# Gelu of four early tiles kept in DRAM until its step, x of the last early tiles loaded sooner, inverse roots of late groups ranked behind normalization

## The chip, the cores and the metric

The kernel runs on one core of a Trainium2 chip. The metric is device time in microseconds (us), the median of the runs. The profile comes from one more execution, recorded by the hardware profiler; its own time is given beside its span.

Engine names in the profile: PE is TensorE's matrix multiplication and PEld its weight load, DVE is VectorE, ACT is ScalarE, POOL is GpSimd, SP is SyncE, which only issues transfers here. A name such as L528 is a line of the kernel.

## The reference

The input x has 4096 rows of 1024 float32 numbers (8 x 512 x 1024). Cut to what matters:

```python
xn   = layernorm(x)                              # each row, eps 1e-5
attn = (w1 @ w2.T) * sparse_mask                 # 1024 x 1024
y    = gelu(xn @ attn + b2)                      # exact gelu; one product, no softmax
w_q  = to_e4m3(weight * 448 / max|weight|)
x_q  = to_e5m2(xn * 57344 / max|xn|)             # one maximum over all of xn
lin  = (x_q @ w_q.T) / x_scale / w_scale + bias
out  = x + y + lin
```

The mask is banded: a column block of 128 needs only rows up to 70 away from it. The scale of the linear layer's input needs the maximum over the whole of xn, so no linear product can start before every row has been normalized or at least measured.

## The kernel before

**Tiles and parts.** The rows are cut into 32 tiles of 128. The first 16 are "early": tile i is loaded once, normalized in place (`normalize` on ACT, L407, or `normalize_gpsimd` on POOL, L416), its row maxima are taken (`row_max`, DVE, L421), PE transposes it in two halves `pt_i_0` and `pt_i_1` (`transpose_one`, L509), ACT or DVE copies them out of PSUM (`evict_transposed` L518, `evict_by_vector` L521), and PE multiplies with the band: `py_i_0` and `py_i_1` (`product_matmul`, L528), each of which must first have been filled with b2 by ACT (`preload`, L525). `gelu_early` (L538) then writes the gelu over the tile of x. Since x itself is gone by then, `add_x` (L541) later fetches it from DRAM once more with an accumulating transfer, which POOL issues. These transfers are released once the gelus and the late maxima (`late_amax`) are done.

The other 16 tiles are "late". In part one they are loaded for their statistics and maxima only: tiles 16 to 23 through a mean and a sum of squares on ACT (`mean_of` L335 and L336, `squares` L339), tiles 24 to 31 through `statistics` on DVE (L330) and a centring on ACT (L349) or POOL (L352). Their slots are given back after the maximum. In part two they are loaded a second time.

**The inverse roots.** 1/sqrt(var) is worked out for groups of tiles (`GROUPS`). Those of tiles 2 to 27 run as eight small operations on POOL (`inverse_root_gpsimd`, L382 to L391), and give `rstd` and `shift` to the normalizations. `root_of_squares` (L397 to L404, POOL) follows the group of 16 to 23. Then `late_amax` and the global maximum of x (PE transposes `pt_x`, L437 and L449) give the scale.

**The weights.** Eight tiles w_0 to w_7 of the linear layer's weight are rounded to fp8 on ACT, DVE (L481, L484) and POOL (L488, L489); a slot becomes free when the second half of its tile has been rounded.

**Part two** starts with the first linear matmul `pf_0_0` (L568) at 132.9 us of the profiled execution. Its steps each take one tile's linear product, in two halves `pf_k_0` and `pf_k_1`, for which there are two PSUM buffers. The products and transposes of the late tiles lie between the linear matmuls. For each half, `total` on DVE scales `pf` and adds the bias (L580), and adds the result to the tile (L583). For an early tile L583 needs the accumulating transfer of `add_x` to have landed; for a late tile it needs POOL's `add_gelu` (L553). `store` issues the output's transfer from ACT's queue. Eight tiles of the mask (`load_mask`) are also read in part two and checked to be zero outside the band (`check_mask`, L604).

**What sets the order.** Every operation is registered with a class `Plan`: engine, planned cost, a rank (the lower goes first among those ready), what it comes after, and which pools it takes from or gives back to. A simulated clock on the planned costs then yields one fixed order for each engine, and the program is emitted in it. Each engine works strictly through its list. An operation placed early waits where it stands, with everything behind it on its engine, whatever the real time is.

The pools that matter are `slot`, 34 tiles of SBUF that hold x, w1, w, xnt, gelu and mask alike, and `stream`, which limits how many late tiles of part one (and mask tiles) are in SBUF at a time. A load waits on SP's queue until its slot is free, with the loads behind it. The order of the loads in part one is written by hand:

```python
ORDER = "eeaaeeeaeeeoaoooooooeeaaesseaesalellssleselllssl"
```

`e` is the next early tile, `s` the next of the late tiles 16 to 23, `l` the next of 24 to 31, `a` the next block of w1, w2 and mask, `o` the next weight tile.

Of the kernel before, what the change touches and what calls it, by code (L numbers as in the profile page):

```python
# [8 lines left out]
F32 = mybir.dt.float32  # L9
# [8 lines left out]
P = 128  # L18
D = 1024
# [4 lines left out]
EARLY = 16  # L24
SLOTS = 34
QUANT = 4
STREAM = 9
LATE = 4

SQUARED = range(EARLY, EARLY + 8)  # L30
# [1 line left out]
BY_SCALAR = (0, 2, 3, 8, 10, 14)  # L32
CENTRED_BY_GPSIMD = range(24, 30)
GROUPS = [(0, 1), (1, 2), (2, 8), (8, 12), (12, 16), (16, 24), (24, 28), (28, 32)]
BY_HALVES = 0
TINY = 1e-36
HALF = 512
# [35 lines left out]

ORDER = "eeaaeeeaeeeoaoooooooeeaaesseaesalellssleselllssl"


def load_order():
# [67 lines left out]
class Plan:  # L147
# [8 lines left out]
    def do(self, engine, cost, rank, emit, *args, lag=0.2, after=(), take=(), free=()):  # L156
        after = [op for op in after if op is not None]
        op = Op(engine, cost, rank, lag, after, take, free, emit, args)
        self.ops.append(op)
        return op  # L160
# [47 lines left out]
def banded_path(  # L208
# [12 lines left out]
    nc = tc.nc  # L221
# [5 lines left out]
    slots = ctx.enter_context(tc.tile_pool(name="slots", bufs=SLOTS))  # L227
    magic_pool = ctx.enter_context(tc.tile_pool(name="magic", bufs=2))
    small = ctx.enter_context(tc.tile_pool(name="small", bufs=2))
    ps_y = ctx.enter_context(tc.tile_pool(name="ps_y", bufs=4, space=psum))  # L230
    ps_f = ctx.enter_context(tc.tile_pool(name="ps_f", bufs=2, space=psum))
    ps_t = ctx.enter_context(tc.tile_pool(name="ps_t", bufs=2, space=psum))
# [5 lines left out]
    def slot(name):  # L238
        return slots.tile([P, D], F32, tag="s", name=name)
# [21 lines left out]
    xs = {}  # L261
# [11 lines left out]
    v = {}  # L273
# [266 lines left out]
    def add_x(i):  # L540
        nc.gpsimd.dma_start(xs[i], x[i * P : (i + 1) * P, :], accum_op=ALU.add)  # L541

    def normalize_late(i):
        xns[i] = slot(f"xn_{i}")
        normalize(i, xns[i])
# [83 lines left out]
    do = plan.do  # L629
    LOAD, T, V, A, G = "load", "tensor", "vector", "scalar", "gpsimd"  # L630
# [21 lines left out]
    for sc in range(NC):  # L652
        mm = do(
            T, 3.6, sc * 0.1, attn_matmuls, sc, after=[attn_ops[c] for c in range(sc + 1)],
            take=("f",), free=("slot",),
# [16 lines left out]
    for lo, hi in GROUPS:  # L672
        group = [stat[i] for i in range(lo, hi)]
        if 0 < lo and hi < TILES:
            op = do(G, 1.9 + 0.18 * (hi - lo), 0, inverse_root_gpsimd, lo, hi, after=group)
        else:
            op = do(V, 0.2, 0, variance, lo, hi, after=group)
            op = do(G, 0.4 + 0.18 * (hi - lo), 0, power, lo, hi, after=(op,))
            op = do(V, 0.6, 0, inverse_root, lo, hi, after=(op,))
        for i in range(lo, hi):  # L680
            root[i] = shifted[i] = op
        if lo == 0 or hi == TILES:
            op = do(V, 0.2, 0 if lo == 0 else 99, shifts, lo, hi, after=(op,))
            for i in range(lo, hi):
                shifted[i] = op
# [9 lines left out]
    for i in range(EARLY, TILES):  # L695
# [8 lines left out]
        after=[maxima[i] for i in SQUARED] + [root[i] for i in SQUARED],  # L704
# [3 lines left out]
        after=[squared] + [maxima[i] for i in range(TILES)] + [root[i] for i in range(TILES)],  # L708
# [19 lines left out]
    for c in range(NC):  # L728
        rank = 5, 4.0, 5.0
        op = do(A, 1.17, rank[0], weight_scaled, c, after=(w_known, w_twice[c]))  # L730
# [5 lines left out]
    known = do(V, 0.2, 0.5, descale, after=(x_known,))  # L736

    products, added = {}, {}
    evicted = {}
    for i in range(EARLY):  # L740
        in_big = i >= EARLY - NC
        for q in range(2):
            op = do(
                T, 0.52, 10 * i - 11 + q, transposes, i, q,
                after=(settled[i], attn_mm[NC - 1] if in_big else None, evicted.get((i, 0))),
                take=("t",) if in_big or q else ("t", "slot"),
            )
            engine, cost, emit = (V, 0.7, evict_by_vector) if q and i in BY_VECTOR else (A, 0.6, evict_transposed)
            evicted[i, q] = do(engine, cost, -2.0, emit, i, q, after=(op,), free=("t",))
        pre = [  # L750
            do(A, 0.62, 1.5 + 0.01 * i, preload, i, h, after=(b2_op,), take=("y",)) for h in range(2)
        ]
        op = evicted[i, 1]
        ends = []
        for piece in band_pieces():
            op = do(
                T, max(0.39, (piece[3] - piece[2]) / 600), 10 * i, product_matmul, i, *piece, lag=0.1 if not piece[-1] else 0.2,
                after=(op, evicted[i, 0], attn_ready[piece[0]], pre[piece[1]]),
            )
            if piece[-1]:  # L760
                ends.append(do(A, 0.62, 0, gelu_early, i, piece[1], after=(op, maxima[i]), free=("y",)))
        products[i] = op

        op = do(LOAD, 2.5, 200 + 10 * i, lambda: None, lag=0.0, after=(*ends, late))
        added[i] = do(G, 1.0, 6 + 0.01 * i, add_x, i, after=(op,), lag=4.0)
# [24 lines left out]
    for s, pair in enumerate(steps):  # L790
        rank = 1000 + 10 * s
        j, nxt = product_in.get(s), turned_in.get(s)
        for k, h in pair:
            if k < EARLY and k not in quantized:
                quantized[k] = do(
                    V, 0.95, 9 + s, quantize, k,
                    after=(x_known, products[k], evicted[k, 1], ends[s - 2] if s > 1 else None),
                    take=("quant",), free=("slot",) if k < EARLY - NC else (),
                )

        op = linear
        for kind, args in interleaved(pair, j is not None, nxt is not None):
            if kind == "product":
                h = args[1]
                op = do(
                    T, 0.335, rank, product_matmul, j, *args, lag=0.0,
                    after=(op, evicted_late[j, 0], evicted_late[j, 1], pre_late[j, h]),
                )
                if args[-1]:
                    last_piece[j, h] = op  # L810
            elif kind == "transpose":
                c, = args
                q, first, last = c // (NC // 2), c % (NC // 2) == 0, c % (NC // 2) == NC // 2 - 1
                op = do(
                    T, 0.13, rank, transpose_one, nxt, c, lag=0.0, after=(op, normal_late[nxt]),
                    take=(("t", "slot") if c == 0 else ("t",)) if first else (),
                    free=("slot",) if c == NC - 1 else (),
                )
                if last:
                    evicted_late[nxt, q] = do(  # L820
                        A, 0.6, 50 + s, evict_transposed, nxt, q, after=(op,), free=("t",)
                    )
            else:
                k, h, c = args
                op = do(
                    T, 0.215, rank, linear_matmul, k, h, c, lag=0.0,
                    after=(op, quantized[k], *(rounded if c == 0 else ())),
                    take=("f",) if c == 0 else (), free=("quant",) if (h, c) == (1, NC - 1) else (),
                )
                if c == NC - 1:  # L830
                    sums[k, h] = op
        linear = op
        ends.append(op)
        if j is not None:
            for h in range(2):
                g = do(
                    A, 0.62, 20 + s, gelu_late, j, h, after=(last_piece[j, h],),
                    take=() if h else ("slot",), free=("y",),
                )
                added_late[j, h] = do(  # L840
                    G, 1.3, 20 + s, add_gelu, j, h, after=(g,), free=("slot",) if h else ()
                )
            quantized[j] = do(
                V, 0.95, 30 + s, quantize, j, after=(x_known, last_piece[j, 0], last_piece[j, 1]),
                take=("quant",), free=("slot",),
            )
        for k, h in pair:
            ready = added_late[k, h] if k >= EARLY else added[k]
            if s == len(steps) - 1:
                op = do(G, 1.3, 20 + s, add_bias, k, h, after=(ready, bias_op))  # L850
                op = do(V, 0.8, 10 + s, total_at_once, k, h, after=(op, sums[k, h], known), free=("f",))
                totals[k, h] = op
            else:
                totals[k, h] = do(
                    V, 1.48, 10 + s, total, k, h, after=(sums[k, h], known, bias_op, ready), free=("f",)
                )
            if s == len(steps) - 1:
                do(A, 0.1, 90, store, k, h, after=(totals[k, h],), lag=4.0)
            elif h == 1:
                stored.append(  # L860
                    do(A, 0.1, 90 + s, store, k, after=(totals[k, 0], totals[k, 1]), lag=4.0,
                       free=("slot",) if k < EARLY else ("slot", "late"))
                )
# [307 lines left out]
```

## Time and profile before

| | us |
|---|---|
| median of 3 runs (lowest to highest) | 321.80 (321.66 to 323.01) |
| the profiled execution | 321.68 |
| its span | 319.8 |
| PE busy | 294.8 |
| DVE, ACT, POOL busy | 232.0, 161.9, 138.0 |
| first linear matmul | 132.94 |

The mean granted clock of PE in the profiled execution is 0.982 of full speed. 69.55 MB are moved in the span.

The profile's page has busy times, the span in 40 slices of 8 us with a digit for the busy tenths of each engine and for the clock granted to PE, the transfer queues (q0 is POOL's, q1 SP's, q10 ACT's), and groups of instructions. The trace behind it answers closer questions: waits by engine and line, a timeline of an engine's instructions (start in us from the span's start, duration, and in brackets how long the engine stood idle before it and for whom), busy times in chosen stretches, and the time from issue to landing of a transfer. A row of the timeline may join neighbouring instructions of one line.

### The profile page before, as it was taken

How to read it: one execution, taken by the hardware profiler on the slowest of the kernel's cores; microseconds unless marked ns; L12 is line 12 of the kernel's file. 1: busy time of each engine (PE TensorE's matmuls, PEld its weight loads, DVE VectorE, ACT ScalarE, POOL GpSimd, SP SyncE). 2: the span in 40 equal slices, each digit the busy share in tenths (PEclk: the TensorE clock that was granted, in tenths of full speed). 3: DMA queues.
4: the chain of work that ended last, by engine and by line, in shares of the span. 5: the costliest groups of instructions: out<-in, count | busy, mean ns of one | idle time of the engine just before them, and what ended most of it. 6: DMA issues, size and time to landing. Idle time of an engine off the chain costs nothing.

```text
span 319.8 us, 4317 instructions
## 1 busy us (share of the span) xinstructions
PE 294.8 (92%) x1530; PEld 217.9 (68%) x1549; DVE 232.0 (73%) x339; ACT 161.9 (51%) x262; POOL 138.0 (43%) x165
## 2 busy tenths in 40 slices
PE   5687879899996899999999999999999999999992
PEld 1665758698894799876766676676667667666651
DVE  3657798899899896358668677767857767676682
ACT  1131578998994799943335244523533452451110
POOL 2402705999998958367443311311321231131160
PEclk9989999999999699999999999999999999999999
DMA  7999999954754190999999999755335223212313
GB/s 243 353 378 380 407 365 388 305 201 167 296 178 151 36 339 20 174 178 225 278 290 307 308 307 372 279 178 184 147 131 198 98 100 133 91 66 107 133 67 139
DMA packets 27693, 69.55 MB, mean 217 GB/s; under 512 B 3344, under 2 KB 12048, under 8 KB 27664
## 3 DMA queue, kind: packets, MB, share of 16 engines
q1 hardware_dynamic: 20320, 42.98, 38.4%
q0 software_dynamic: 2592, 9.44, 14.7%
q10 hardware_dynamic: 4752, 16.78, 13.2%
q8 instruction: 14, 0.23, 0.3%
q14 instruction: 15, 0.12, 0.1%
HBM read 52.41 MB, written 16.78 MB: 216 GB/s over the span
## 4 chain that ended last, share of the span: by engine, by line
PE 64%; DMA 11%; POOL 11%; DVE 6%; SPq 3%; issue 2%; ACT 1%; POOLq 0%; DVEq 0%
PE pf L568 33%; PE py L528 25%; DMA w_sb<-in_w2t_dram 7%; PE pt L509 5%; POOL wq L489 3%; POOL w L488 3%; DMA w<-in_wt_dram 3%; DVE st L330 2%; DMA w<-in_w_dram 2%; DVE magic L481 1%; SPq L290 1%; PE pa L313 1%; DVE magic L484 1%; POOL x L416 1%; POOL g_r L384 1%
## 5 line engine op out<-in xcount | busy, mean ns | idle before, releaser
L568 PE MATMUL pf<-wq,xqts 128*128 128x512 bf16 x493 | 145.6, 379 | 0.8
L528 PE MATMUL py<-attn,xnt 128*128 128x198 f32 (+2 forms) x480 | 114.0, 341 | 2.4 <-ACT py L525 1.2
L528 PEld LDWEIGHTS py<-attn,xnt 128*128 128x128 f32 x480 | 86.8, 190 | 25.2 <-ACT py L525 2.1
L553 POOL TENSOR_TENSOR x<-x,gelu 128x512 f32<-128x512 f32 x32 | 40.7, 1271 | 125.4 <-ACT gelu L550 118.2
L580 DVE SCALAR_TENSOR_TENSOR pf<-pf,descale,bias_bc 128x512 f32<-128x512 f32 x62 | 46.9, 757 | 52.6 <-PE pf L568 50.1
L568 PEld LDWEIGHTS <-xqts 128*128 128x128 fp8e5 x512 | 50.6, 101 | 25.9 <-DVE xqts L561 2.7
L550 ACT ACTIVATE gelu<-py 128x512 f32<-128x512 f32 x32 | 19.1, 597 | 77.9 <-PE py L528 67.5
L518 ACT COPY xnt<-pt 128x512 f32<-128x512 f32 x48 | 27.9, 586 | 37.1 <-PE pt L509 36.3
L583 DVE TENSOR_TENSOR x<-pf,x 128x512 f32<-128x512 f32 x62 | 42.9, 691 | 4.0
L313 PE MATMUL pa<-w_sb,w 128*128 128x268 f32 (+1 forms) x128 | 32.0, 410 | 8.5 <-DMA w_sb<-in_w2t_dram 8.5
L421 DVE TENSOR_REDUCE row_amax<-x 128x1 f32<-128x1024 f32 x32 | 37.6, 1204 | 1.7 <-POOL x L416 1.6
L525 ACT COPY py<-b_bc 128x512 f32<-128x512 f32 x64 | 37.0, 596 | 0.9
L313 PEld LDWEIGHTS pa<-w_sb,w 128*128 128x128 f32 x128 | 26.0, 211 | 14.4 <-issue 6.3
L330 DVE BATCH_NORM_STATS2 st<-x 128x6 f32<-128x512 f32 x48 | 30.2, 671 | 7.5 <-DMA x<-in_x_dram 7.5
L528 PE MATMUL py<-attn,xnt_big 128*128 128x198 f32 (+2 forms) x160 | 34.2, 358 | 0.1
L509 PE MATMUL pt<-ident,xn 128*128 128x128 f32 x128 | 34.0, 273 | 0.2
L528 PEld LDWEIGHTS py<-attn,xnt_big 128*128 128x128 f32 x160 | 28.3, 203 | 2.4
L509 PEld LDWEIGHTS pt<-ident,xn 128*128 128x128 f32 x128 | 17.9, 141 | 14.3 <-ACT xnt L518 0.6
L488 POOL TENSOR_TENSOR w<-w,magic 128x512 f32<-128x512 f32 x16 | 18.9, 1182 | 14.3 <-DVE magic L484 13.9
L509 PE MATMUL pt<-ident,x 128*128 128x128 f32 x128 | 19.8, 283 | 5.4 <-DVE xnt_big L521 2.7
L561 DVE TENSOR_SCALAR xqts<-xnt,x_scale 128x1024 fp8e5<-128x1024 f32 x24 | 24.5, 1026 | 0.0
L509 PEld LDWEIGHTS pt<-ident,x 128*128 128x128 f32 x128 | 14.9, 146 | 9.2 <-DVE xnt_big L521 3.2
(87 smaller groups left out, 233.6 us busy)
## 6 DMA issues: line engine op xcount, KB each, us to landing
x<-in_x_dram SPq DMA_DIRECT2D x48, 512.0 KB, 5.9
out_dram<-x ACTq DMA_DIRECT2D x31, 512.0 KB, 3.3
x<-in_x_dram POOLq DMA_DIRECT2D x16, 512.0 KB, 12.8
w<-in_wt_dram SPq DMA_DIRECT2D x8, 512.0 KB, 9.2
mask<-in_mask_dram SPq DMA_DIRECT2D x8, 512.0 KB, 8.0
w<-in_w_dram SPq DMA_DIRECT2D x7, 512.0 KB, 9.5
w_sb<-in_w2t_dram SPq DMA_DIRECT2D x6, 512.0 KB, 10.3
attn<-in_mask_dram SPq DMA_DIRECT2D x6, 134.0 KB, 9.0
```

The costliest lines, as they stand in the source:

```text
L313: nc.tensor.matmul(pt[:, : hi - lo], w1_sb[:, c, :], w2_sb[:, c, lo:hi], start=(c == 0), stop=(c == NC - 1),)
L330: nc.vector.bn_stats(st[:, h, :], xs[i][:, half(h)])
L421: nc.vector.tensor_reduce(row_amax[:, i : i + 1], xs[i], AX.X, ALU.max, apply_absolute_value=True)
L488: nc.gpsimd.tensor_add(w[:, half(h)], w[:, half(h)], magic[:, half(h)])
L509: nc.tensor.transpose(pts[i, q][:, j, :], xn[:, c * P : (c + 1) * P], ident)
L518: nc.scalar.copy(xnts[i][:, q * (NC // 2) : (q + 1) * (NC // 2), :], pts.pop((i, q)))
L525: nc.scalar.copy(pys[i, h], b2_bc[:, half(h)])
L528: nc.tensor.matmul(pys[i, h][:, lo - h * HALF : hi - h * HALF], xnts[i][:, sc, :], attn[:, sc, lo - band(sc)[0] : hi - band(sc)[0]], start ...
L553: nc.gpsimd.tensor_add(xs[i][:, half(h)], xs[i][:, half(h)], gelus[i][:, half(h)])
L568: nc.tensor.matmul(v["pf", i, h], v["quant"][:, xqts[i], c, :], wq[:, c, half(h)], start=(c == 0), stop=(c == NC - 1),)
L580: nc.vector.scalar_tensor_tensor(pf, pf, v["descale"], v["bias"][:, half(h)], ALU.mult, ALU.add)
L583: nc.vector.tensor_add(res[:, half(h)], pf, res[:, half(h)])
```

## The change

The diff has three parts and one size that goes with them.

1. `ORDER` has two early tiles (x_14, x_15) further ahead: they are loaded right after x_13, and tiles 25, 26, 19, 20 and those that follow come after them. `STREAM` goes from 9 to 10.
2. For the early tiles 4 to 7 (`SPILLED`) the gelu does not stay in SBUF. After both gelus of the tile, `spill` writes it to DRAM (issued by ACT), and its slot is free. Four steps ahead of the tile's own step, `unspill` takes a slot and loads it again (issued by SP), and `add_x`, the accumulating transfer on POOL, comes after that. These are eight more transfers of 512 KB.
3. The rank of `inverse_root_gpsimd` goes from 0 to 3 for the groups of late tiles (16 to 23 and 24 to 27), the rank of the normalizations.

```diff
-STREAM = 9
+STREAM = 10
...
+SPILLED = range(4, 8)
...
-ORDER = "eeaaeeeaeeeoaoooooooeeaaesseaesalellssleselllssl"
+ORDER = "eeaaeeeaeeeoaoooooooeeaaesseaesaleeellsslslllssl"
...
+    spilled = ctx.enter_context(tc.tile_pool(name="spilled", bufs=1, space=bass.MemoryType.DRAM))
...
+    def spill(i):
+        v["spilled", i] = spilled.tile([P, D], F32, tag=f"spilled_{i}", name=f"spilled_{i}")
+        nc.scalar.dma_start(v["spilled", i], xs.pop(i))
+
+    def unspill(i):
+        xs[i] = slot(f"x_{i}")
+        nc.sync.dma_start(xs[i], v.pop(("spilled", i)))
...
-            op = do(G, 1.9 + 0.18 * (hi - lo), 0, inverse_root_gpsimd, lo, hi, after=group)
+            op = do(G, 1.9 + 0.18 * (hi - lo), 0 if lo < EARLY else 3, inverse_root_gpsimd, lo, hi, after=group)
...
-    evicted = {}
+    evicted, away = {}, {}
...
+        if i in SPILLED:
+            away[i] = do(A, 0.1, 0, spill, i, after=ends, lag=4.0, free=("slot",))
+            continue
...
+        for k in SPILLED:
+            if (k, 0) in steps[min(s + 4, len(steps) - 1)]:
+                op = do(LOAD, 1.4, 185 + 5 * s, unspill, k, lag=2.0, take=("slot",), after=(away[k], ends[s - 1]))
+                added[k] = do(G, 1.0, 6 + 0.01 * k, add_x, k, after=(op,), lag=4.0)
```

What the new lists hold, as emitted: on SP, x_14 and x_15 follow x_13, then x_25, x_26, x_19, x_20, x_27; four of the second-pass and part-two loads are preceded by the reload of a spilled tile. On ACT the mean of x_19 stands ahead of the preload of `py_6_0`, and the squares of x_23 stand behind the eviction of `pt_15_0`. On POOL the roots of 12 to 15 come after the second half of w_5, the root of 24 to 27 after the normalization of x_15, and the accumulating transfers go in the order 0, 1, 2, 3, 8 to 14, 4, 15, 5, 6, 7. PE's and DVE's orders in part two are the same as before.

## The prediction

> **What bounds the kernel now.** I read the page's busy rows first, then the waits, then the stretches in which TensorE is not full.
>
> ```profile
> PE 294.8 (92%) x1530; PEld 217.9 (68%) x1549; DVE 232.0 (73%) x339; ACT 161.9 (51%) x262; POOL 138.0 (43%) x165
> PE   5687879899996899999999999999999999999992
> PEclk9989999999999699999999999999999999999999
> ```
>
> TensorE is busy for 294.8 of 319.8 us, and from about 115 us on without a hole. So a change can win only in the holes ahead of that: the loads at the start, which the diff doesn't touch, and slices 13 and 14 (97 to 112 us), where PE falls to 6 and 8 and the clock row to 6. The waits of 95 to 106 us name the first:
>
> ```profile
> ACT x L407 <- POOL shift L391: 4.5, 1, 4.5
> PE pt L509 <- DVE xnt_big L521: 2.7, 1, 2.7
> PE pt L509 <- POOL x L416: 1.7, 1, 1.7
> ```
>
> ScalarE stood 4.5 us at the normalization of x_14, for the inverse root of tiles 12 to 15, and the evictions behind it were late; then PE stood for x_12, normalized on GpSimd. GpSimd's timeline says why x_12 was late (start, duration, line):
>
> ```profile
> 97.79 0.20 POOL L382 TENSOR_SCALAR g_var<-mean_var 128x4 f32<-128x4 f32 x1
> ...
> 100.92 0.19 POOL L382 TENSOR_SCALAR g_var<-mean_var 128x4 f32<-128x4 f32 x1
> ...
> 103.94 2.39 POOL L416 TENSOR_SCALAR x<-x,rstd,shift 128x1024 f32<-128x1024 f32 x2
> ```
>
> The group of 12 starts at 97.79, and the group of 24, wanted by nobody soon, goes ahead of x_12 for 3.02 us (100.92 to 103.94). The hole has a second price, seen in three stretches of 3.41 us (duration, PE busy, ..., clock):
>
> ```profile
> 99.99:103.40 3.41, 0.87 (x6) 0.69 (x6) 3.34 (x7) 2.53 (x4) 2.66 (x9) 1.00 0.45 154
> 103.40:106.82 3.42, 1.76 (x9) 1.63 (x9) 1.85 (x3) 3.39 (x8) 3.30 (x5) 0.50 0.02 5
> 106.82:110.23 3.41, 3.41 (x11) 2.97 (x11) 3.41 (x4) 2.87 (x6) 3.33 (x4) 0.50 0.00 0
> ```
>
> After a stretch with 0.87 us of work the clock is granted at 0.50, until one full stretch has gone by at 110.23.
>
> **The change part by part.** *Removed.* The two PE waits, 2.74 + 1.66 = 4.40 us. Behind them 105.19 to 110.23 ran at half clock: 5.04 us for 2.5 us of work. Together **-6.9**. That it goes: in the new order x_14 and x_15 are loaded with the batch that follows w_2's rounding at 72.75, so the statistics of x_15 are done near 89, not 96.4. GpSimd runs the group of 12 after w_5 (91.1 to 94.1), one half of w_6, then x_12, done near 97.8; PE wants it near 104. The group of 24 (3.0 us) now lies behind x_15 and ahead of w_7, all in GpSimd's slack.
>
> *Wait A, the mean of x_19.* SyncE's queue issues loads in the written order. x_19 used to go out at 73.20 and landed at 77.40. Now x_14, x_15, x_25 and x_26 stand ahead, and x_26 waits for the slot of w_3, whose rounding ends at 78.01. So x_19 takes the place of the load issued at 78.5:
>
> ```profile
> L278 SPq DMA_DIRECT2D x<-in_x_dram x1: 350/350/350, 78.5 to 78.5; - x1
> DMA to landing us min/median/max: 4.2/4.2/4.2
> ```
>
> It lands near 82.65. ScalarE's order does not follow the load:
>
> ```profile
> 77.48 1.06 ACT L335 ACTIVATE x<-x 128x1024 f32<-128x1024 f32 x1 [0.79 <-DMA x<-in_x_dram]
> ```
>
> This is the mean of x_19, which waited for its load already before. In the new order behind it on ScalarE stand the preload of py_6_0 (L525), the squares of x_19 and the gelus of tiles 4 and 5. The mean starts at 82.7, takes 1.29 (with its accumulator read and the scaling), the preload 0.60: py_6_0 is ready at 84.67 and PE wants it at 81.12. **+3.55**, 1 us per us of lateness; nothing if x_19 lands by 79.2.
>
> *The clock after A: which rule?* The rows: stretches with 0.87 (above) and with 1.06 us of work (11.24 to 14.66) were followed by half clock, one with 1.96 (28.31 to 31.72) was not. If the stretches stay on the raster of this trace, 81.68 to 85.09 would hold 0.42 us of work: half clock for one stretch, which costs 3.41 / 2 = 1.7. The Trainium skill, "TensorE: Matmul & The Clock Gate", Part 1, has the clock fall after at least one idle window of about 3.4 us, with windows that run free of the program. Read strictly, a hole of 3.55 us covers a whole window only by chance and costs nothing (sum 323.4). The rows show a drop after a window that was not empty, so I take the row, **+1.7** (sum 325.1); ends 0 and 3.4 (two stretches, as at 103.40).
>
> *Wait B, the x scale.* In the new ScalarE order the squares of x_23 stand behind the eviction of pt_15_0, which PE must first make; before, they were not behind a late transpose. The chain from there:
>
> ```profile
> 119.28 0.19 POOL L382 TENSOR_SCALAR g_var<-mean_var 128x8 f32<-128x8 f32 x1 [1.97 <-ACT x L339]
> ...
> 124.39 1.67 POOL L399 TENSOR_TENSOR r_squares<-row_amax,neg_half 128x8 f32<-128x8 f32 x1
> ```
>
> After pt_15_0: eviction 0.8, squares 1.35, hand-over 0.1, root of 16 to 23 (119.28 to 122.98) 3.70, root of squares 3.15 (124.06 to 127.19; group 28's power now goes ahead of it elsewhere), maxima of the rows 0.7: 9.8 us. The products that PE has between pt_15_0 and the transpose pt_x (L437) are 8.16 us. So PE stands about 1.65 there, and with pf_0_0 behind quantize 0.3 more: **+1.95**. Ends 0 (it was hidden before) and 3.
>
> *Spill.* Four stores (ScalarE issue, 512 KB) at 87 to 98 us, where the DMA share is 0.3 to 0.8; the page has a store landing in 3.3 us. They end 50 us before the reload. ScalarE pays 0.03 to 0.35 for an issue, in slack. Two issues wait for earlier landings in their queues, with gelus behind them, but these loads are early by then. **0**; if that cover fails, 4 x 0.35 = 1.4.
>
> *Wait C, x_4's add.* Part two is already full of transfers. From 120 to 200 us:
>
> ```profile
> q0 software_dynamic: 2352, 8.53, 55.7%
> q1 hardware_dynamic: 1584, 5.77, 19.1%
> ```
>
> Queue 0 is the sixteen accumulating loads of L541; it takes 2.6 us a tile when alone (x_0 to x_3) and about 5.0 later. Queue 1 is SyncE's: 11 tiles in 19.1% of 80 us, so 1.39 us of the engines each. In the new GpSimd order the adds run 0 to 3, 8 to 14, 4, 15, 5, 6, 7: x_4 moves from fifth to twelfth. With P the first linear matmul (132.94), the twelfth landed at 176.27 = P + 43.3. The queue starts 2.6 us later against P (wait B delays the late maxima that release it), and three to four more loads go by on SyncE in that time (x_4, x_5, x_6 back, x_20 sooner), 4.9: P + 50.8. Needed:
>
> ```profile
> 178.22 0.76 DVE L580 SCALAR_TENSOR_TENSOR pf<-pf,descale,bias_bc 128x512 f32<-128x512 f32 x1 [1.94 <-PE pf L568]
> 179.02 0.69 DVE L583 TENSOR_TENSOR x<-pf,x 128x512 f32<-128x512 f32 x1
> ```
>
> The second row is the sum of tile 4, at P + 46.1. The two pf buffers give 1.7 of slack, so PE stands 50.8 - 47.8: **+3.0**. Ends 0 and 5. x_5 (fourteenth, P + 61 against 59 + 3), x_6 and x_7 then fit, and so do the late loads x_22 and x_23. Here again a rule weighs against the change: the skill's "DMA: Bandwidth & Descriptors", section "Queues, rings and completion order", has each engine take turns between queues packet by packet, so the accumulating queue cannot keep its rate when loads join. The trace agrees (2.6 us a tile alone, 5.0 with company); with the lone rate C would be 0 and the sum 322.1.
>
> **Sum.** On the profiled execution, 321.68 (span 319.8): -6.9 + 3.55 + 1.7 + 1.95 + 3.0 = +3.3, so 325.0. The median of the runs, 321.80, is 0.1 above it: **325.1**.
>
> **The rivals.** *C is hidden*: the reloads lie in gaps, or the adds keep up; then 322.1, and 320.4 if the clock also holds. For it: the DMA row of the page counts waiting packets as busy, and what queue 0 gains from fewer competing stores isn't shown; against it: shares near 1.0 from 133 us to 200. *Faster*: A is the mechanism. If x_19 lands by 79.2 (3.4 us sooner than I place it), PE meets no wait there and keeps its clock, and 325.1 - 3.55 - 1.7 = 319.9. For it: a load alone took 3.2 us; against it: its issue stands behind w_3's rounding, which ends at 78.01, so it would have to land 1.2 us after. Partial earliness of 2 us gives about 321.5. *The change doesn't do what it says*: ScalarE's and GpSimd's delay from A carries on until x_12 is late all the same; then 332. Against it: 6 us of slack at x_12. *Worse C*: the queue falls 5 us behind and PE's hole trips the clock once more (1.7): 328.8.
>
> **How the numbers follow.** 0.5% is 1.6 us, about what a measurement of this kernel can tell from no change: 320.2 to 323.4. The sum as it stands, 0.50 (own range 323.4 to 327.5); C hidden 0.24 (a fifth of it under 320.2); A absent 0.12; worse C 0.10; x_12 late 0.04. Faster: 0.12 less a little, plus 0.04: 0.15. Slower: 0.50 + 0.10 + 0.04, less a little where B and C are both at their low end: 0.60. Same: 0.25. The range leaves out the deep end of the fast case and the last two tails: 319.5 to 328.6.
>
> **What would show it.** Right: no PE wait on POOL x L416 and clock 1.0 near 100 to 110 us; ScalarE waiting 4 us for x at L335 near 79 us with PE waiting for py L525 just after, and half clock behind it; PE waiting at pt_x near 127; DVE's L583 waiting for the accumulating load near 180 us, PE behind it. Wrong: a PE row without the hole at 81 us (x_19 was early), or a total of tile 4 that never waits. Most damaging would be an order of transfers other than first in, first out on SyncE's queue, since A and C both rest on it.

## The result

The changed kernel took 327.69 us (median of 4 runs, 326.07 to 327.92), the kernel before 322.40 beside it: ratio 1.0152, 95% interval 1.0107 to 1.0198. A longer series (the first experiment below, 20 runs against 41) gave 326.64 against 322.86, ratio 1.0091, interval 1.0065 to 1.0116. Of the 20 runs of the longer series the six above 327.9 us, the one that was profiled among them, are more than 1.5% over the fastest: the ratio leaves them out and the median does not (without them it is 325.76). Where later profiles are set against the changed kernel, its first profile is meant. It is slower, as forecast: the forecast was 325.1, or +3.3 us; the first series says +5, the longer one +3 to +4.

The page of the changed kernel, busy rows and slices (the span is now 326.0 us):

```profile
PE 297.8 (91%) x1530; PEld 219.4 (67%) x1549; DVE 228.4 (70%) x339; ACT 161.8 (50%) x262; POOL 138.4 (42%) x165
PE   5769869899699999999999996999999999999993
PEclk9789987999899999999999997999999999999997
```

The dip of PE that was in slices 13 and 14 is gone. In its place are one in slice 11 (about 82 to 90 us) and one in slice 25 (about 196 to 204 us), each with a dip of the clock. Closer, in stretches of 3.41 us where the clock changed and one of 15 us where the old hole was (duration, PE busy, PEld, DVE, ACT, POOL, clock, transfer share, GB/s):

```profile
83.45:86.86 3.41, 0.34 (x2) 0.34 (x3) 3.34 (x6) 2.23 (x5) 3.25 (x4) 1.00 0.73 258
86.86:90.27 3.41, 3.41 (x10) 2.87 (x9) 3.41 (x4) 2.78 (x6) 2.91 (x3) 0.50 1.02 390
95.00:110.00 15.00, 15.00 (x93) 13.97 (x92) 13.61 (x20) 14.36 (x27) 13.75 (x23) 1.00 0.89 295
...
196.07:199.49 3.42, 0.59 (x4) 0.24 (x2) 2.79 (x5) 0.00 (x0) 0.44 (x1) 1.00 1.06 319
199.49:202.90 3.41, 3.13 (x9) 1.52 (x9) 2.25 (x4) 1.71 (x2) 0.00 (x0) 0.50 1.03 358
```

95 to 110 us is full, at full clock. Both new holes are followed by one stretch at 0.50. The waits of 78 to 92 us name the first (total, times, longest):

```profile
ACT x L337 <- DMA x<-in_x_dram: 3.4, 1, 3.4
...
PE py L530 <- ACT py L527: 3.2, 1, 3.2
```

That is wait A as it was drawn: ScalarE at the mean of x_19, which landed at 84.51, and PE at py_6_0 behind it. The second hole is in part two, but not at the instruction that I named. VectorE's timeline there (start, duration, idle before it):

```profile
191.86 0.69 DVE L593 TENSOR_TENSOR x<-pf,x 128x512 f32<-128x512 f32 x1
196.67 1.00 DVE L614 TENSOR_REDUCE out_cols<-mask 128x1 f32<-128x186 f32 x2 [4.12 <-DMA mask<-in_mask_dram]
```

and PE's:

```profile
199.77 1.01 PE L578 MATMUL pf<-wq,xqts 128*128 128x512 bf16 x2 [3.11 <-DVE x L593]
```

VectorE stood 4.1 us for the third mask tile, with the second sum of tile 5 queued behind it, and PE had no free pf buffer.

A single execution says less than one would like. The program is the same up to the products of tile 3, yet in the fourteen profiles of this study (kernel before, changed kernel, twelve experiments) they began between 68.05 and 71.31 us. Until then they had run 3.4 to 13.7 us at half clock; how much of the spread that makes is not shown (e12 had 10.2 us of it and began at 68.41, e11 had 6.8 and began at 71.28). So I cut each profile in three, worked out from its PE rows: the start (to the first product of tile 3), part one (from there to the first linear matmul of tile 1), part two (from there to the end of the span).

| profile | start | part one | part two | median of runs | ratio to before (95%) |
|---|---|---|---|---|---|
| before | 68.64 | 71.57 | 179.58 | 322.40 | |
| changed | 70.95 | 70.46 | 184.55 | 327.69 | 1.0152 (1.0107 to 1.0198) |
| e1, changed again | 71.31 | 70.18 | 184.73 | 326.64 | 1.0091 (1.0065 to 1.0116) |
| e2, x_19's mean later | 70.46 | 72.71 | 184.76 | 328.43 | 1.0181 (1.0143 to 1.0219) |
| e3, mask check later | 69.79 | 70.20 | 181.59 | 324.62 | 1.0058 (1.0028 to 1.0087) |
| e4, three moves | 68.10 | 73.32 | 179.71 | 323.99 | 1.0034 (1.0010 to 1.0058) |
| e5, and spill of 7 later | 70.07 | 69.96 | 181.70 | 323.11 | 1.0025 (1.0005 to 1.0044) |
| e6, x_19's mean, spill of 7 | 69.94 | 71.24 | 181.93 | 324.62 | 1.0075 (1.0047 to 1.0103) |
| e7, before with root of 24 later | 70.25 | 68.77 | 179.77 | 319.69 | 0.9908 (0.9883 to 0.9934) |
| e8, changed, no spill | 69.50 | 71.61 | 179.73 | 322.51 | 0.9996 (0.9978 to 1.0015) |
| e9, e8 with x_19's mean later | 68.05 | 70.18 | 179.80 | 321.19 | 0.9977 (0.9951 to 1.0002) |
| e10, e7 with x_14 later | 68.21 | 69.55 | 179.44 | 319.76 | 0.9913 (0.9894 to 0.9933) |
| e11, e7 with eviction sooner | 71.28 | 69.11 | 179.65 | 320.16 | 0.9915 (0.9885 to 0.9944) |
| e12, e11 with x_14 later | 68.41 | 72.82 | 179.49 | 321.42 | 0.9960 (0.9940 to 0.9980) |

The change's own part in the first profile is -1.1 in part one and +5.0 in part two, +3.9 us; the other 2.3 us of the difference of spans are the start.

### The profile page after: what moved, and what is told of

Read it like the earlier page. It is cut to its first block, busy times and chain, and to the rows that moved or that the text cites. A ratio compares the mean times of both kernels' runs of the same rounds, so it can differ in the third digit from the quotient of the medians.

```text
span 326.0 us, 4329 instructions
## 1 busy us (share of the span) xinstructions
PE 297.8 (91%) x1530; PEld 219.4 (67%) x1549; DVE 228.4 (70%) x339; ACT 161.8 (50%) x262; POOL 138.4 (42%) x165
## 5 line engine op out<-in xcount | busy, mean ns | idle before, releaser
L578 PE MATMUL pf<-wq,xqts 128*128 128x512 bf16 x493 | 147.3, 382 | 4.1 <-DVE x L593 3.4
L530 PE MATMUL py<-attn,xnt 128*128 128x198 f32 (+2 forms) x480 | 115.7, 344 | 5.5 <-ACT py L527 4.3
L530 PEld LDWEIGHTS py<-attn,xnt 128*128 128x128 f32 x480 | 88.4, 193 | 28.0 <-ACT py L527 4.9
L590 DVE SCALAR_TENSOR_TENSOR pf<-pf,descale,bias_bc 128x512 f32<-128x512 f32 x62 | 46.9, 757 | 50.8 <-PE pf L578 48.4
L578 PEld LDWEIGHTS <-xqts 128*128 128x128 fp8e5 x512 | 50.8, 101 | 30.0 <-issue 4.5
L520 ACT COPY xnt<-pt 128x512 f32<-128x512 f32 x48 | 27.9, 585 | 33.3 <-PE pt L511 29.1
L315 PE MATMUL pa<-w_sb,w 128*128 128x268 f32 (+1 forms) x128 | 35.0, 435 | 8.6 <-DMA w_sb<-in_w2t_dram 8.4
L315 PEld LDWEIGHTS pa<-w_sb,w 128*128 128x128 f32 x128 | 27.5, 224 | 15.6 <-issue 8.5
L530 PE MATMUL py<-attn,xnt_big 128*128 128x198 f32 (+2 forms) x160 | 31.4, 342 | 0.0
L530 PEld LDWEIGHTS py<-attn,xnt_big 128*128 128x128 f32 x160 | 26.6, 190 | 2.2
L409 ACT ACTIVATE xn<-x,shift,rstd 128x1024 f32<-128x1024 f32 x16 | 19.8, 1244 | 6.4 <-DMA x<-in_x_dram 6.4
L543 POOL DMA_DIRECT2D x<-in_x_dram x16 | 14.9, 1134 | 14.9 <-DVE x L593 8.6
```

The lines of the kernel that those rows point to most:

```text
L315: nc.tensor.matmul(pt[:, : hi - lo], w1_sb[:, c, :], w2_sb[:, c, lo:hi], start=(c == 0), stop=(c == NC - 1),)
L520: nc.scalar.copy(xnts[i][:, q * (NC // 2) : (q + 1) * (NC // 2), :], pts.pop((i, q)))
L530: nc.tensor.matmul(pys[i, h][:, lo - h * HALF : hi - h * HALF], xnts[i][:, sc, :], attn[:, sc, lo - band(sc)[0] : hi - band(sc)[0]], start ...
L578: nc.tensor.matmul(v["pf", i, h], v["quant"][:, xqts[i], c, :], wq[:, c, half(h)], start=(c == 0), stop=(c == NC - 1),)
L590: nc.vector.scalar_tensor_tensor(pf, pf, v["descale"], v["bias"][:, half(h)], ALU.mult, ALU.add)
```

## The experiments

**e1: the changed kernel again.** No edit.

> The changed kernel once more, unchanged, for what varies by itself. In its first profile it was already 2.3 us behind the kernel before when the first product of tile 3 began (70.95 against 68.64 us), and the program is the same up to there. Theory (the stretches of the clock fall differently on the loads of the start in each execution): another profile shows another start, the products of tile 3 anywhere from 68 to 72 us, and everything behind it the same holes: about 3 us at py_6_0, 1 us at pt_x, 3 us near 199. Rival (the new program itself starts later): tile 3 at 71 us again. Median 326 to 328 us either way.

Tile 3 began at 71.31, holes of 2.86 at py_6_0, 1.13 at pt_x and 3.20 at 199.86. By itself this left both readings open. The experiments that follow share the start: those built on the changed kernel began tile 3 at 68.05 to 70.46, those on the kernel before at 68.21 to 71.28. So the late start does not belong to the new program, and the same holes came again.

**e2: the mean of x_19 behind the preloads.** For this and the later moves the planned order is taken and single operations are put behind others before the program is emitted; the lines of these kernels are shifted by it, and by the change. The edit:

```diff
     def emit(self):
-        for op in self.order():
+        order = self.order()
...
+        for what, behind in MOVED:
+            op = order.pop(at(*what))
+            order.insert(at(*behind) + 1, op)
...
+        for op in order:
             op.emit(*op.args)
...
+MOVED = [(("mean_of", 19), ("preload", 7, 0)), (("squares", 19), ("mean_of", 19)),
+         (("row_max_late", 19), ("squares", 19))]
```

Here `at` finds an operation's place in the order by its name and tile.

> The changed kernel with the mean and squares of x_19 four places later on ScalarE, behind the preloads of py_6_0, py_6_1 and py_7_0 (the maximum of its rows goes behind one statistics on VectorE). Theory (wait A): the hole of 3.2 us at py_6_0 goes, and the half clock behind it (1.7 us): 322.8 us, 4.9 less than the changed kernel. Rival (the lateness of x_19 is only passed on, since its squares, the slot that they free and all behind it are as late as before): the hole reappears further on, 326 to 328 us. If the clock's loss is not tied to the hole: 324.5.

328.43 us: no gain, and part one 2.3 us longer than in the first profile of the changed kernel. The hole at py_6_0 was gone, but one of 4.42 us stood at py_9_1 (102.67). What made it is clearer in e4, which has the same hole. The rival was right: the hole reappeared further on.

**e3: the check of the third mask tile later.**

```diff
+MOVED = [(("check_mask", 2), ("total", 20, 1))]
```

> The changed kernel with the check of the third mask tile five places later on VectorE, behind both sums of tile 20. Theory (VectorE stands 4.1 us for the mask tile, which the reload of x_7 pushed back, and holds the sums of tile 5): the PE hole of 3.1 us near 199 us goes, and the half clock behind it (1.7 us): 322.9 us. Rival, the one that I had predicted (the accumulating transfers are late as such): VectorE stands at the sum of tile 5 or 6 instead, and 2 us or more of the hole remain: 326 us.

324.62 us, part two 3.0 shorter than in the changed kernel. The hole of 3.1 us and its half clock went. What is left there are holes of 0.54 (pf of tile 19) and 1.13 us (py_22_0, for a tile loaded late). VectorE's wait for an accumulating load in this stretch was 1.2 us, at tile 4. So the mask tile held PE; the adds as such cost half a microsecond. The gain is less than the 4.8 us that I expected, because of the holes that are left, and by the ratios alone it is not clear of e1 (the intervals overlap): the reading rests on the trace, and on e8.

**e4: both moves, and the squares of x_23 sooner.**

```diff
+MOVED = [... the four of e2 and e3 ..., (("squares", 23), ("mean_of", 23))]
```

> The changed kernel with three moves: mean and squares of x_19 later, the check of the third mask tile later, and the squares of x_23 seven places earlier on ScalarE, behind the mean of x_23. Theory: the three holes of PE and the two stretches of half clock were all that the change cost, so 327.7 - 4.9 - 4.8 - 1.4 = 316.6 us, about the kernel before less the 7.0 us of its own hole with its clock. Rival (the holes hide others that come out once they are gone, as the adds of the reloaded tiles or the later evictions): 319 to 323 us.

323.99 us. Part two is as short as without a spill (179.71), the wait at pt_x is gone, but part one is 3.1 longer than in e3. ScalarE's timeline of e4 shows the reason:

```profile
95.38 1.06 ACT L559 ACTIVATE x<-py 128x512 f32<-128x512 f32 x2
99.82 0.33 ACTq L566 DMA_DIRECT2D spilled<-x  x1
100.19 1.11 ACT L546 COPY py<-b_bc 128x512 f32<-128x512 f32 x2 [3.75 <-DMA x<-in_x_dram]
```

and PE's waits of 93 to 106 us:

```profile
PE py L549 <- ACT py L546: 5.0, 1, 5.0
```

The issue of tile 7's spill is made to wait until x_29 has landed, and ScalarE, which issues it, stood there 3.75 us with the preload of py_9_1 behind it. In the changed kernel the same issue waited for nothing. It looks as if wait A had hidden a second wait for the same loads, and so I read it before e5. But x_29 itself left later. SyncE's waits of 74 to 104 us, in the changed kernel and then in e4:

```profile
SPq L280 <- POOL g_var L384: 3.6, 1, 3.6
SPq L280 <- DVE row_amax L423: 3.2, 1, 3.2
```

```profile
SPq L299 <- POOL g_var L403: 7.2, 1, 7.2
```

In the changed kernel x_28 left at 89.11, right behind a row maximum on VectorE, and x_29 at 92.87, right behind the rounding of w_5 on GpSimd (the view names L384, GpSimd's next instruction). In e4 x_28 left behind the rounding of w_5 (90.59) and x_29 behind that of w_6 (96.57). The move had taken the maximum of x_19 along, which gives a slot back, and the loads behind it came to wait for later slots. Counted from the start of tile 3, x_29 left after 27.9 to 28.5 us in the five experiments that move x_19 (e2, e4, e5, e6, e9) and after 21.9 to 22.5 us without the move (the changed kernel, e1, e3, e8). In the changed kernel it landed after 25.9 us, in e4 after 31.7; ScalarE was free for the spill of e4 after 28.3. By these figures the second wait was made by the way in which I took the first one away. Whether x_19's mean can go later with the loads left in time, no run shows.

**e5: the spill of tile 7 moved too.**

```diff
+MOVED = [... the five of e4 ..., (("spill", 7), ("squares", 21))]
```

> The last kernel (three moves) and a fourth: the spill of tile 7 goes from ahead of the preload of py_9_1 on ScalarE to behind the squares of x_21. In the last run ScalarE stood 3.75 us at that spill, which waits for x_29 to land, and PE 5.0 us for py_9_1 behind it, then 6.8 us at half clock. Theory (the changed kernel has two waits of ScalarE for the same late loads in a row, the second in the shadow of the first): without both, PE has no hole over 1 us from 60 us on, 324.0 - 5.0 - 3 = 316 us. Rival (the inverse root of group 12, for which ScalarE stood 2 us in the last run at the normalization of x_14, or x_12, is what comes next): a hole of 2 to 4 us remains between 95 and 108 us, 319 to 321 us.

323.11 us. Part one is 3.4 shorter than in e4, only 0.5 shorter than in the changed kernel. Up to pt_x PE now had holes of 0.67, 0.57, 1.76 (pt_13_1) and 1.96 us (pt_x), with no half clock; 4.95 us of idle time in all. The rival's place was wrong (not 95 to 108 us), its point was right: other waits come out. The larger one is at pt_x, for the maxima: PE came sooner, the x scale hardly did (pt_x ran 59.3 us after the start of tile 3, against 59.8 in the changed kernel and 62.3 in e4).

**e6: only the two moves on ScalarE.**

```diff
+MOVED = [... the three of e2 ..., (("spill", 7), ("squares", 21))]
```

> Only the two moves on ScalarE that belong to late loads: mean and squares of x_19 behind the preload of py_7_0, and the spill of tile 7 behind the squares of x_21. Theory: the changed kernel (326.6 in its longer series) loses its hole of 3 us at py_6_0 with its clock and gets no other: 321.9 us, with the holes at pt_x and near 199 us left. Rival (lateness is passed on to a third place): 325 us or more.

324.62 us, holes of 1.71 at pt_13_1 and 1.94 at pt_x: lateness passed on to a third place. Against e1 it is 2 us by the medians; by the ratios the intervals overlap (1.0047 to 1.0103 and 1.0065 to 1.0116), so how much of A is really to be had stays open. x_29 left late here too.

**e7: the kernel before with the root of tiles 24 to 27 later.**

```diff
+MOVED = [(("inverse_root_gpsimd", 24, 28), ("normalize_gpsimd", 15))]
```

> The kernel before with one thing of the change alone: GpSimd's inverse root of tiles 24 to 27 goes behind the normalization of x_12, x_13 and x_15. Theory (the PE wait of 1.7 us for x_12 was made by that root; the wait of 2.7 us ahead of it came from ScalarE at x_14, which this does not touch): -1.7 us, and the half clock, which the first hole alone sets off, stays for the most part: 321 us against 322.9. Rival (x_12 is not what PE waits for, since the tile's transposes follow a late eviction): no difference.

319.69 us, 0.9908: 3.0 us by the ratio, more than I expected, and the best of all kernels here. PE's timeline:

```profile
103.62 0.66 PE L524 MATMUL pt<-ident,x 128*128 128x128 f32 x4 [2.56 <-DVE xnt_big L536]
104.12 0.50 PE L543 MATMUL py<-attn,xnt_big 128*128 128x198 f32 x2
104.45 0.60 PE L524 MATMUL pt<-ident,x 128*128 128x128 f32 x4
```

x_12's transposes follow without a pause where 1.66 us had been, and in this profile no stretch ran at half clock behind the hole of 2.56 (before: two). The clock is luck in part: here the hole lay across two stretches,

```profile
98.83:102.24 3.41, 2.23 (x11) 1.63 (x10) 3.34 (x8) 0.28 (x1) 2.66 (x9) 1.00 0.45 167
102.24:105.66 3.42, 2.04 (x16) 2.01 (x17) 3.39 (x5) 3.42 (x7) 3.38 (x3) 1.00 0.17 65
```

while in e10 below a hole of 2.79 us lay mostly in one,

```profile
99.54:102.95 3.41, 0.61 (x6) 0.58 (x6) 3.34 (x7) 2.59 (x5) 2.99 (x6) 1.00 0.45 154
```

and a stretch at half clock followed. A new hole of 1.37 us came at the transposes of x_14. This is the third part of the diff alone, as far as it concerns the group of 24 to 27, and it beats both kernels.

**e8: the change without the spill.**

```diff
-SPILLED = range(4, 8)
+SPILLED = range(0)
```

> The changed kernel without the spill (no tile is spilled; order of loads, the size of the stream pool and the rank stay). Theory: wait A stays, since x_19 is loaded in the same place, 3 us and its clock; the reloads and with them the hole of 3.2 us near 199 us and its half clock go, and no issue of a spill stands on ScalarE: 326.6 - 4.9 = 321.7 us. Rival (the slots that the spill frees are what lets the later loads go in time): x_30, x_22, x_23 and x_16 to x_18 wait for weights and maxima again, PE gets holes between 110 and 133 us, 324 us or more.

322.51 us, ratio 0.9996. Part two 179.73, 4.8 shorter than in the changed kernel, so the spill costs 4.8 us there. Part one is that of the kernel before: wait A stands alone, in the waits of 78 to 92 us

```profile
ACT x L337 <- DMA x<-in_x_dram: 3.9, 1, 3.9
...
PE py L530 <- ACT py L527: 3.6, 1, 3.6
```

with two stretches at half clock behind it, and eats what the root's rank wins. The rival's holes between 110 and 133 us did not come (the largest is 0.39). The late loads do go later without the spill (x_30 by 6 us, counted from the start of tile 3), but PE does not feel it.

**e9: e8 with x_19's mean later.** Edit as in e2, on the kernel of e8.

> The changed kernel without the spill, and with the mean and squares of x_19 behind the preload of py_7_0 on ScalarE. Without the spill it took 322.5 us and PE still stood 3.6 us at py_6_0, with 6.8 us at half clock. Theory (that hole is made by ScalarE alone, and it was the issue of a spill that made a new one out of it in the earlier run): the hole goes and no other over 2 us comes, 322.5 - 3.6 - 3 = 316 us. Rival (the hole moves to x_14's root or x_29's load as before): 319 us or more.

321.19 us. The hole of 3.6 us was gone with its half clock and nothing over 1.03 us came, but there were seven holes of 0.25 to 1.03, 3.94 us of idle from tile 3 to pt_x against 4.18 in e8. The idle time was spread, not removed; the clock was won. By the ratios it is not clear of e8. x_29 left 5.7 us later than in e8, so this is not wait A taken away by itself either. Neither expectation holds in full.

**e10: e7 with the normalization of x_14 later.**

```diff
+MOVED = [... that of e7 ..., (("normalize", 14), ("mean_of", 22))]
```

> The kernel before, with the root of tiles 24 to 27 behind the normalizations of x_12, x_13 and x_15 on GpSimd, and the normalization of x_14 on ScalarE behind the mean of x_22, six places later; loads, pools and spills as before. Theory (ScalarE at x_14 made the hole of 2.7 us, the root of tiles 24 to 27 that of 1.7; neither needs an earlier load): both holes go, 319.7 - 2.6 = 317 us. Rival (x_13 and x_15, or the maxima behind them, are late as such without the earlier loads, as the 1.4 us that appeared at the transposes of x_14 say): 319 us.

319.76 us, as e7. ScalarE no longer waited for the root, and PE's hole was still there. Waits of 93 to 106 us, and the load of the engines from 91 to 101.7 (same columns as above):

```profile
PE pt L532 <- DVE xnt_big L544: 2.8, 1, 2.8
```

```profile
91.00:101.70 10.70, 8.58 (x54) 7.65 (x52) 10.49 (x19) 9.59 (x20) 9.33 (x14) 1.00 0.58 196
```

VectorE is busy 10.49 of 10.70 us. In the kernel before it is the same (10.51), and its timeline shows what stood ahead of the eviction (L521) for which PE waited:

```profile
99.01 1.28 DVE L330 BATCH_NORM_STATS2 st<-x 128x6 f32<-128x512 f32 x2
100.32 0.21 DVE L331 BATCH_NORM_AGGREGATE mean_var<-st 128x2 f32<-128x12 f32 x1
100.45 1.23 DVE L330 BATCH_NORM_STATS2 st<-x 128x6 f32<-128x512 f32 x2
101.71 0.21 DVE L331 BATCH_NORM_AGGREGATE mean_var<-st 128x2 f32<-128x12 f32 x1
101.84 0.64 DVE L521 COPY xnt_big<-pt 128x512 f32<-128x512 f32 x1
```

The statistics of two late tiles, in VectorE's own queue. So the first of the two old holes was not ScalarE's at x_14, as I had read it.

**e11: e7 with that eviction ahead of the statistics.**

```diff
+MOVED = [... that of e7 ..., (("statistics", 28), ("evict_by_vector", 10, 1)),
+         (("statistics", 29), ("statistics", 28))]
```

> The kernel before, with the root of tiles 24 to 27 behind the normalizations of x_12, x_13 and x_15 on GpSimd, and on VectorE the eviction of pt_10_1 ahead of the statistics of x_28 and x_29 instead of behind them. The last run had ScalarE free of its wait at x_14, and the hole of 2.8 us at the transposes pt_11_1 stood as before, with VectorE busy without a pause. Theory (VectorE's own queue makes that hole: the eviction that frees the buffer stands 2.7 us behind statistics that nobody waits for): the hole goes, 319.7 - 2.6 = 317 us. Rival (ScalarE at x_14, 4.3 us, is the second wait for the same place, as its evictions stand behind it): a hole of 1 to 4 us stays near 102 us, now for ScalarE, 319 us.

320.16 us (0.9915, as e7). The hole at pt_11_1 went, and one of 2.00 us came at pt_12_0, for an eviction of ScalarE, which now stood 4.4 us at x_14. The rival was right.

**e12: e11 with x_14 later too.** Both moves together.

> The same with the normalization of x_14 also moved on ScalarE, behind the mean of x_22. Theory: with neither VectorE's statistics nor ScalarE's normalization ahead of the evictions PE has no hole over 1 us from 60 to 200 us: 317 us, or 315.5 if no stretch runs at half clock behind 100 us. Rival (the hole is passed on to x_14's own transposes): 319 us.

321.42 us, slower than e7: 1.48 us at pt_12_0 for x_12 itself, and 2.84 at the transposes of x_14, with two stretches at half clock. The hole was passed on once more.

## Why the prediction was right, and where its steps failed

The direction and the range held, and the range was wide (9.1 us). The sum was +3.3, the change's own part in the first profile +3.9. That these lie so near is in part luck: the terms of part one make +0.3 where -1.1 was measured, that of part two +3.0 where +5.0 was, and the two errors offset. By its steps:

- *Removed, -6.9.* Held in the changed kernel: 4.40 us of waits and 6.8 us of half clock are gone. The reason given for the first hole was wrong (e10): VectorE's queue made it, not ScalarE's wait at x_14. In the changed kernel PE's order has the transposes of tile 10 ahead of 40 more products, and VectorE copied pt_10_1 out 25.3 us after the start of tile 3 and not 33.2, ahead of those statistics. For the second hole, the root of tiles 24 to 27 ahead of x_12, the reason holds (e7).
- *Wait A, +3.55.* Measured 3.16, in the place named, and of the named cause, for x_19 landed at 84.51 after an issue at 80.26. Whether it is a cost that can be taken away is open: the move that removed it in e2 and e4 also sent x_28 and x_29 out later, and PE lost 4.4 and 5.0 us at py_9_1 for it.
- *The clock, +1.7 by the row, 0 by the strict rule.* The row was right, twice: stretches with 0.34 and with 0.59 us of PE work were followed by one at half clock. What the Trainium skill has under "TensorE: Matmul & The Clock Gate", Part 1, as an idle window need not be an empty one here. But the row is not a sharp line either: this stretch of the changed kernel's start was followed by half clock, with as much work as the second one of e7 above, which was not.

```profile
42.48:45.89 3.41, 2.04 (x13) 1.08 (x11) 3.38 (x7) 1.94 (x4) 0.00 (x0) 1.00 1.12 345
```

- *Wait B, +1.95.* 1.13 us at pt_x and 0.31 just behind it: 1.44. Moving the squares of x_23 took the wait at pt_x away in e4, but there PE also came later.
- *Spill, 0.* The stores do lie beside other work. The cover that I named for the issue on ScalarE, "these loads are early by then", held: x_29 landed at 96.80, and the issue that needs it came at 100.54. Without wait A too: in e4 ScalarE came to that issue 28.3 us after the start of tile 3, still behind the 25.9 at which x_29 had landed in the changed kernel. But the price where the cover fails was wrong: in e4, with x_29 late, it cost 5.0 us of PE and not 1.4.
- *Wait C, +3.0.* The step that failed; that its size was nearly met is luck. The sum of tile 4 waited 1.2 us on VectorE and cost PE 0.30: the adds were less late than worked out, x_4 landing 47.1 us after the first linear matmul and not 50.8. I charged 4.9 us for the passing loads where the trace has 1.9 (3.8 later in all, of which the queue's own start was 1.9, not 2.6). And I followed the reloads past GpSimd's queue only. On SyncE's queue the mask tiles stand behind them, and those I did not list. The transfer of the third mask tile, before and then after:

```profile
L298 SPq DMA_DIRECT2D mask<-in_mask_dram x1: 328/328/328, 169.4 to 169.4; - x1
DMA to landing us min/median/max: 14.6/14.6/14.6
```

```profile
L300 SPq DMA_DIRECT2D mask<-in_mask_dram x1: 417/417/417, 177.4 to 177.4; - x1
DMA to landing us min/median/max: 19.3/19.3/19.3
```

Counted from the first linear matmul (132.94 and 134.14) it was issued 6.8 us later, behind the reload of x_7, which waited for out_17 to be stored, and it took 4.7 us longer. The check of it on VectorE is wanted by nobody, but the sums behind it are. PE lost 3.11 and half a stretch of clock, 1.7: +4.8 where I had 3.0. e3 and e8 show both that it was this wait and that the reloads made it.

That lateness is handed from one engine to the next in part one is shown (e11, e12; in e2 and e4 to e6 the move of x_19 made part of it); that VectorE, with 10.5 busy microseconds of 10.7, is the floor under all of these orders, is argued from it and not shown by a run of its own. The time of A that could be had with the spill in place stays open (e6), since every run that moved x_19's mean also sent x_29 out late.

## What to carry to other kernels

Where a scheduler writes one fixed order for each engine, cost a moved or added transfer against every queue that it is put into, and list what stands behind it there, also work that nobody waits for: a check that waits in order holds the work behind it. Before a hole is priced as a gain, ask what else its engine would meet if it came sooner, and before a hole is moved away, ask what the moved operations give back: here a slot came back later, two loads left about 4 and 6 us later, and a new hole stood behind them. Split a change into its parts early; here one rank was worth -0.9%, the reordered loads took that back, and the spill cost 1% on top.

## What the runs showed of the hardware

- The clock of PE changed on a raster of 3.41 us. Counted on this raster in the fourteen profiles, all 30 full-clock stretches with less than 1.45 us of PE work were followed by one at half clock, 14 of the 35 with 1.45 to 2.05 us, and none of the 1148 with more. Behind the hole at 86.52 us one full stretch brought the clock back.
- How these stretches lie on the program differs from run to run: a hole of 2.56 us cost no half clock in e7, one of 2.79 us a stretch in e10. The runs of one kernel lay between 323.06 and 328.35 us (e1); what made each of them long or short is not shown.
- A transfer's issue on ScalarE can wait for an unrelated load to land, and it holds the engine's arithmetic while it does: 3.75 us in e4. In this trace the landing of x_29 and that of the waiting spill are told by the same semaphore.
